# A graph layer on one core: both halves of a table from one matmul, four groups of raw rows, and the sum ahead of the node matrix

## The chip, the cores and the metric

The kernel runs on one core of a Trainium2 chip. The metric is the device time of one execution in microseconds; before the change it is 1374.2 us, the median of three runs (1370.36 to 1376.34).

## What is computed

One message-passing layer on a graph of N = 6250 nodes and E = 100000 edges, with H = 128 features and 4 attributes an edge, all in float32. The edges are sorted by destination. Cut to what matters:

```python
msg_in = concatenate([x[src], x[dst], edge_attr], axis=1)      # E x 260
h = silu(msg_in @ mW1 + mb1)                                   # E x 128
messages = h @ mW2 + mb2
aggregated = segment_sum(messages, dst, num_segments=N)        # N x 128
u = silu(concatenate([x, aggregated], axis=1) @ uW1 + ub1)
y = layer_norm(x + (u @ uW2 + ub2), ln_g, ln_b)
out = layernorm(x + y)
```

The kernel splits mW1 by rows: 128 for the source node, 128 for the destination node, 4 for the attributes. So `msg_in @ mW1` is a row of a table `x @ mW1[:128]` picked by src, plus a row of a table `x @ mW1[128:256] + mb1` picked by dst, plus a small product of the attributes. mW2 is applied after the sum over edges, folded into uW1.

## The kernel before, in words

**Groups.** Edges are worked on in groups of 1024, eight tiles of 128 edges: 98 groups. Nodes are worked on in batches of 4 tiles of 128 nodes, 13 in all, the last two shorter, each started once all edges into it are done.

**Tables.** Before the loop, TensorE transposes x, part by part (eight tiles of 128 nodes a part, seven parts, the last of one tile; `turn_x`, L325), and multiplies it with the two halves of mW1 (`product`, L318, called for part 1 at L338 and for part 0 at L341). Each call fills one PSUM buffer of 128x1024 (`wide`, three buffers in turn) with eight matmuls of 128 columns. VectorE adds mb1 to the one and SyncE's queue writes it to `tab_b` in device memory; ScalarE copies the other, which goes to `tab_a`. VectorE also clears the accumulators `acc` and `deg` (L344, L345). At 49 tiles and two halves that is 98 matmuls; the profile counts two passes each.

**Gathers.** GpSimd fetches source rows with one indirect DMA for each tile of 128 edges (`fetch`, L263, issued at L268), eight a group, into six buffers `ga`. The first RAW = 5 groups are fetched from x itself, as the tables aren't there yet; their product with mW1[:128] is made on TensorE in the loop (L563 transposes, L554 matmuls). All later groups come from `tab_a`, so the first of them waits for the last write of that table. In iteration g the loop issues the fetch of group g + 4; it can run when the buffer of group g - 2 is free, that is, when that group's rows have been read.

**The loop's iteration g** (L593 on). The program order, which is also the order on each engine's queue, since the scheduling is by hand:

- SyncE: load the destination rows of group g + 4 (`mv`, a window of 96 rows of `tab_b`) and its attributes (`st`).
- VectorE, L527 (`node_matrix`, group g + 3): a 96x1024 matrix of zeros and ones, destination window against edge, from a list of 8-bit numbers; with it, the number of edges of each node.
- TensorE, L552 (`products`, group g + 2): that matrix and the attributes times `mv`, into a PSUM buffer `pre`.
- VectorE, L570 (`hidden`, group g): `s` = gathered rows + `pre`. It is the last reader of the gather buffer. ScalarE, L571: `h` = silu(`s`).
- VectorE, L540 (`edge_matrix`, group g + 1): `oh`, edges against the window of 96, for the sum.
- TensorE, L577 and L580 (`by_nodes`, group g - 1): counts transposed, then `h` times `oh`, summed over the eight tiles into the PSUM tile `held_ps`. `oh` reads a constant row that is kept in `held_ps` too, and TensorE's L577 waits for VectorE's `oh`.
- VectorE, L586 (`add`, group g - 2): `held_ps` added into `acc` and `deg` at the window's place. It waits for TensorE's `by_nodes` just before it in the program.
- One step of each node batch that is running (`node_batch`, L394 on): matmuls, silu, two layer norms, mostly on VectorE (L411, L412, L448, L450, L457, L460) and ScalarE.

For a group of the first RAW, L565 copies the transposed rows out of PSUM in place of the sum. When iteration RAW begins, the products of three groups are made at once.

Of the kernel before, what the change touches and what calls it, by code (L numbers as in the profile page):

```python
# [8 lines left out]
F32 = mybir.dt.float32  # L9
# [9 lines left out]
P = 128  # L19
# [5 lines left out]
def kernel(  # L25
# [40 lines left out]
    nc = tc.nc  # L66
    N, H = x.shape
# [4 lines left out]
    G = 8  # L72
    GE = G * P
    NG = -(-E // GE)
# [4 lines left out]
    RB = 14  # L79
    AHEAD = 4  # L80
    LEAD = 4
    RAW = 5
    MADE = 3
    NQ = 4
    NM = 5
# [11 lines left out]
    def groups(n, g):  # L97
        return [(i, min(g, n - i)) for i in range(0, n, g)]
# [13 lines left out]
    def wide():  # L112
        return ps.tile([P, G, P], F32, name="pre", bufs=3)
# [5 lines left out]
    tpool = tables.enter_context(tc.tile_pool(name="tables", bufs=1, side="right"))  # L119
# [25 lines left out]
    x_sb = tpool.tile([P, NT, H], F32, name="x_sb")  # L145
    nf = N // P
    w1 = consts.tile([P, 2, H], F32, name="w1")
    src_l = by_group(src, 0)
    nc.scalar.dma_start(w1, mW1[: 2 * H].rearrange("(s k) f -> k s f", k=P))
    b1 = consts.tile([P, H], F32, name="b1")  # L150
# [11 lines left out]
    mv = [consts.tile([K1, H], F32, name=f"mv{k}") for k in range(NM)]  # L162
# [91 lines left out]
    tab_a = dram.tile([NP, H], F32, name="tab_a")  # L254
    tab_b = dram.tile([NW, H], F32, name="tab_b")
# [4 lines left out]
    def tiles_of(g):  # L260
        return min(G, -(-(E - g * GE) // P))

    def fetch(g):  # L263
        if g >= NG:
            return
        rows[g] = gath.tile([P, G, H], F32, name="ga")
        for i in range(tiles_of(g)):
            nc.gpsimd.indirect_dma_start(  # L268
                out=rows[g][:, i, :],
                out_offset=None,  # L270
                in_=x if g < RAW else tab_a[:, :],
                in_offset=bass.IndirectOffsetOnAxis(
                    ap=src_i[:, g, i : i + 1] if g else src_0[:, i : i + 1], axis=0
                ),
            )

    for g in range(RAW):
        fetch(g)
# [30 lines left out]
    xT = consts.tile([P, NP], F32, name="xT")  # L309

    def by_node(t):
        return t[:NP].rearrange("(i p) f -> p i f", p=P)
# [2 lines left out]
    nc.vector.memset(zeros, 0.0)  # L315
    nc.sync.dma_start(tab_b[NP:NW], zeros)

    def product(i0, n, part):  # L318
        pm = wide()
        for i in range(n):  # L320
            cols = slice((i0 + i) * P, (i0 + i + 1) * P)
            nc.tensor.matmul(pm[:, i, :], xT[:, cols], w1[:, part, :], start=True, stop=True)  # L322
        return pm[:, :n]

    def turn_x(i0, n):  # L325
        pt = wide()
        for i in range(n):
            nc.tensor.transpose(pt[:, i, :], x_sb[:, i0 + i, :], ident)
        nc.scalar.copy(xT[:, i0 * P : (i0 + n) * P], pt[:, :n, :].rearrange("p i f -> p (i f)"))
# [3 lines left out]
    for k, (i0, n) in enumerate(parts):  # L333
        if k + 1 < len(parts):
            turn_x(*parts[k + 1])

        t = x_sb[:, i0 : i0 + n, :]
        nc.vector.tensor_add(t, product(i0, n, 1), b1[:, None, :].to_broadcast([P, n, H]))  # L338
        nc.sync.dma_start(by_node(tab_b)[:, i0 : i0 + n, :], t)
        t = tpool.tile([P, G, H], F32, name="t", bufs=2)  # L340
        nc.scalar.copy(t[:, :n], product(i0, n, 0))  # L341
        nc.sync.dma_start(by_node(tab_a)[:, i0 : i0 + n, :], t[:, :n])
        cols = slice(i0 * P, NW if i0 + n == NT else (i0 + n) * P)
        nc.vector.memset(acc[:, cols], 0.0)  # L344
        nc.vector.memset(deg[:, cols], 0.0)  # L345
# [23 lines left out]
    def load_weights():  # L369
        for name, shape in (("w2", [P, H]), ("u1a", [P, H]), ("mb2", [P, 1])):  # L370
            raw_w[name] = work.tile(shape, F32, name=f"raw_{name}", bufs=1)
        nc.sync.dma_start(raw_w["w2"], mW2)
        nc.sync.dma_start(raw_w["u1a"], uW1[P:])
        nc.sync.dma_start(raw_w["mb2"], mb2.rearrange("(f o) -> f o", o=1))
        nc.sync.dma_start(u1x, uW1[:P])
        nc.sync.dma_start(u2, uW2)
        nc.sync.dma_start(ub1_col, ub1.rearrange("(f o) -> f o", o=1))
        nc.sync.dma_start(ub2_row, ub2.rearrange("(o f) -> o f", o=1))
        for t, row in ((g_b, ln_g), (b_b, ln_b)):
            nc.sync.dma_start(t, row.rearrange("(o f) -> o f", o=1).to_broadcast([P, H]))  # L380

    def fuse_weights():
        pt = narrow()
        nc.tensor.transpose(pt[:, :P], raw_w["w2"], ident)
        w2T = work.tile([P, P], F32, name="w2T", bufs=1)
        nc.scalar.copy(w2T, pt[:, :P])
        pm = narrow()
        nc.tensor.matmul(pm[:, :H], w2T, raw_w["u1a"], start=True, stop=True)
        nc.tensor.matmul(pm[0:1, H:], raw_w["mb2"], raw_w["u1a"], start=True, stop=True)
        nc.scalar.copy(w2u, pm[:, :H])  # L390
        nc.scalar.copy(mb2u, pm[0:1, H:])
# [133 lines left out]
    def node_matrix(g):  # L525

        nc.vector.tensor_scalar(  # L527
            stbuf[g % NST][:W],
            near.pop(g),
            p_next,  # L530
            0.0,
            op0=OP.is_equal,
            op1=OP.add,
            accum_out=deg_g[:, g : g + 1],
        )

    def edge_matrix(g):

        oh = work.tile([P, G, W], F32, name="oh", bufs=3)
        nc.vector.tensor_tensor(  # L540
            oh,
            w_row[:, None, :].to_broadcast([P, G, W]),
            rel[:, g, :, None].to_broadcast([P, G, W]),
            op=OP.is_equal,
        )
        return oh

    def products(g, xg=None):
        pre = wide()
        st = stbuf[g % NST].rearrange("k (i c) -> k i c", i=G)  # L550
        for i in range(tiles_of(g)):
            nc.tensor.matmul(pre[:, i, :], st[:, i, :], mv[g % NM], start=True, stop=xg is None)  # L552
            if xg is not None:
                nc.tensor.matmul(pre[:, i, :], xg[:, i, :], w1[:, 0, :], start=False, stop=True)  # L554
        return pre

    def hidden(g):
        h = hbuf[g % NH]
        ga = rows.pop(g)
        if g < RAW:  # L560
            px = wide()
            for i in range(G):
                nc.tensor.transpose(px[:, i, :], ga[:, i, :], ident)  # L563
            xg = work.tile([P, G, P], F32, name="s")
            nc.vector.tensor_copy(xg, px)  # L565
            nc.scalar.activation(h, products(g, xg), AF.Silu)
        else:
            n = tiles_of(g)
            s = work.tile([P, G, H], F32, name="s")
            nc.vector.tensor_add(s[:, :n], ga[:, :n], pre.pop(g)[:, :n])  # L570
            nc.scalar.activation(h[:, :n], s[:, :n], AF.Silu)  # L571
        return h
# [19 lines left out]
    pre, oh, h, pt, running = {}, {0: edge_matrix(0)}, {}, {}, []  # L592
    for g in range(NG + 1):  # L593
        if g == 3:
            load_weights()
        if g == 5:
            fuse_weights()
        for c in range(1, NC):
            if g == max(1, c * EC // GE - 10):
                attributes(c)  # L600
            if g == max(1, c * EC // GE - 10) + 1:
                attribute_rows(c)
        if g + AHEAD >= RAW:
            fetch(g + AHEAD)
        if g + LEAD < NG:
            load(g + LEAD)
        if g + MADE < NG:
            node_matrix(g + MADE)
        if g >= RAW:
            for k in range(g if g == RAW else g + MADE - 1, min(g + MADE, NG)):  # L610
                pre[k] = products(k)
        if g < NG - 1:
            h[g] = hidden(g)
        if g + 1 < NG:
            oh[g + 1] = edge_matrix(g + 1)
        if 0 <= g - 1 < NG:
            pt[g - 1] = by_nodes(g - 1, h.pop(g - 1), oh.pop(g - 1))
        for k in range(max(g - 2, 0), g - 1 if g < NG - 1 else g):
            if k in pt:
                add(k, pt.pop(k))  # L620
        for i0, n, first in batches:
            if g == min(first + 1, NG):
                tiles = node_tiles(nodes, node_ps)
                if first == NG:

                    tiles = (
                        nodes,
                        lambda name, p=P: gath.tile([P, G, H], F32, name="ga")[:p, :BT],
                        lambda: wide()[:, :BT],
                    )  # L630
                running.append(node_batch(i0, n, *tiles))
        advance(running)
        if g >= NG - 2:
            advance(running)
        if g == NG - 1:
            h[g] = hidden(g)
# [157 lines left out]
```

## Time and profile before

| what | value |
|---|---|
| time, median of 3 | 1374.2 us |
| profiled execution | 1372.6 us |
| busy: GpSimd / TensorE matmul / VectorE / ScalarE | 54% / 51% / 35% / 17% |
| gathers: from x, from `tab_a` | 40, 742 |
| first gather of all; last gather from x ends | 4.06 us; 54.15 us |
| first gather from `tab_a` | 88.99 us |
| last gather ends | 1297.96 us |
| matmuls of the tables (L322), passes | 196, mean 307 ns |
| sum `s` (L570), whole group | 92 times, mean 1207 ns |
| node matrix (L527) | 98 times, mean 1262 ns |

How to read it: times are counted from the first instruction. A group's line gives its engine, operation, what it writes and reads, how often, its busy time in all and for one, and after the bar how long the engine stood idle just before it, and what ended that idle time. Busy shares are means over the whole span; no engine is near full, so the order in which engines wait for each other matters more than any of the shares. A GpSimd gather is recorded with 0.95 us, and the next starts 0.30 us after it.

### The profile page before, as it was taken

To read this page: it belongs to the slowest core of one execution; us is meant where nothing else is said; L and a number is where in the kernel's file an instruction comes from. 1 tells how busy PE (TensorE), PEld (TensorE's weight loads), DVE (VectorE), ACT (ScalarE), POOL (GpSimd) and SP (SyncE) were. 2 spreads that over 40 slices of the span, in tenths; PEclk is the share of its full clock that TensorE was granted. 3 is DMA by queue.
4 is the path that set the end of the run, shared out by engine and by line. 5 is a ranking of instruction groups with operands and counts; after the bars stand their busy time and mean duration, and the time that the engine had idled before them with its cause. 6 is when DMAs were issued, how large, how long until landed. Compare 5 with 4: busy or idle time off the path is not lost. (4 is left out here: it accounts for less than half of the span.)

```text
span 1372.6 us, 11511 instructions
## 1 busy us (share of the span) xinstructions
PE 704.8 (51%) x3818; PEld 624.6 (46%) x3818; DVE 477.5 (35%) x1012; ACT 237.4 (17%) x288; POOL 741.4 (54%) x790
## 2 busy tenths in 40 slices
PE   3356743656465355445344543675543664544565
PEld 2356643545355244345234443565433454434453
DVE  1172323324334234234233325234324333225343
ACT  0121101112212112112102201212202202202223
POOL 7435564656456556546645654666655565655400
PEclk8577775755666657656656765656756665766765
DMA  6363222212312222222212221322222222222100
GB/s 168 90 177 83 56 66 65 64 48 57 79 43 67 55 60 70 58 57 70 74 33 68 56 64 41 78 58 74 62 58 58 56 69 64 58 58 56 47 1 28
DMA packets 69917, 88.96 MB, mean 65 GB/s; under 512 B 20671, under 2 KB 51534, under 8 KB 69850
## 3 DMA queue, kind: packets, MB, share of 16 engines
q0 software_dynamic: 25024, 51.30, 15.0%
q1 hardware_dynamic: 41290, 35.08, 9.0%
q10 hardware_dynamic: 3536, 1.77, 0.5%
q8 instruction: 32, 0.52, 0.1%
q14 instruction: 35, 0.29, 0.1%
HBM read 76.71 MB, written 11.38 MB: 64 GB/s over the span
## 5 line engine op out<-in xcount | busy, mean ns | idle before, releaser
L268 POOL DMA_INDIRECT ga<-tab_a,src_i x742 | 702.2, 946 | 541.6 <-DVE s L570 277.8
L552 PE MATMUL pre<-mv,st 100*128 100x128 f32 x1564 | 278.3, 336 | 57.2 <-issue 56.9
L586 DVE TENSOR_TENSOR acc<-acc,held_ps 128x96 f32 x98 | 25.0, 255 | 780.6 <-remote 511.7
L577 PE MATMUL held_ps<-ident,deg_g 96*1 96x96 f32 x98 | 28.6, 292 | 509.6 <-DVE oh L540 482.5
L552 PEld LDWEIGHTS pre<-mv,st 100*128 100x128 f32 x1564 | 257.6, 250 | 69.2 <-issue 68.8
L580 PE MATMUL held_ps<-oh,h 128*128 128x96 f32 x1564 | 287.5, 361 | 0.3 <-ACT h L571 0.3
L580 PEld LDWEIGHTS held_ps<-oh,h 128*128 128x128 f32 x1564 | 276.6, 274 | 1.4 <-ACT h L571 0.7
L577 PEld LDWEIGHTS held_ps<-ident,deg_g 96*1 96x1 f32 x98 | 8.0, 82 | 532.3 <-DVE oh L540 501.9
L571 ACT ACTIVATE h<-s 128x1024 f32<-128x1024 f32 (+1 forms) x93 | 98.1, 1055 | 718.4 <-DVE s L570 653.3
L527 DVE TENSOR_SCALAR_CACHE_REDUCE st<-near,p_next 96x1024 f32<-96x1024 uint8 x98 | 123.5, 1262 | 24.0 <-issue 14.3
L570 DVE TENSOR_TENSOR s<-ga,pre 128x1024 f32<-128x1024 f32 (+1 forms) x93 | 112.0, 1204 | 2.9 <-PE pre L552 2.7
L540 DVE TENSOR_TENSOR oh<-held_ps,rel 128x768 f32<-128x768 f32 x98 | 92.3, 942 | 0.0
L571 ACT ACT_TABLE_LOAD x21 | 26.9, 1283 | 126.0 <-DVE s L570 113.1
L322 PE MATMUL pre<-w,xT 128*128 128x128 f32 x196 | 29.1, 307 | 31.6 <-issue 15.7
L322 PEld LDWEIGHTS pre<-w,xT 128*128 128x128 f32 x196 | 27.4, 222 | 33.5 <-issue 16.0
L268 POOL DMA_INDIRECT ga<-in_x_dram,src_i x32 | 30.3, 946 | 9.8 <-issue 9.8
L554 PE MATMUL pre<-w,s 128*128 128x128 f32 x80 | 22.1, 371 | 18.9 <-DVE s L565 16.3
L417 ACT ACT_TABLE_LOAD x24 | 30.8, 1283 | 2.7 <-DVE mv L412 2.3
L446 PEld LDWEIGHTS y<-u,uT 128*128 128x128 f32 x94 | 22.7, 327 | 15.4 <-issue 15.4
L425 ACT COPY acc_b<-acc 128x512 f32<-128x512 f32 (+1 forms) x12 | 7.3, 609 | 124.3 <-DVE acc L586 115.3
L554 PEld LDWEIGHTS pre<-w,s 128*128 128x128 f32 x80 | 17.8, 275 | 19.9 <-DVE s L565 17.0
L446 PE MATMUL y<-u,uT 128*128 128x128 f32 x94 | 26.0, 448 | 0.0
(117 smaller groups left out, 396.0 us busy)
## 6 DMA issues: line engine op xcount, KB each, us to landing
ga<-tab_a,src_i POOLq DMA_INDIRECT x742
near<-near_d SPq DMA_DIRECT2D x24, 384.0 KB
mv<-tab_b SPq DMA_DIRECT2D x98, 48.0 KB
tab_b<-x_sb SPq DMA_DIRECT2D x6, 512.0 KB
tab_a<-t SPq DMA_DIRECT2D x6, 512.0 KB
xs<-in_x_dram SPq DMA_DIRECT2D x11, 256.0 KB
out_dram<-z SPq DMA_DIRECT2D x11, 256.0 KB
st<-ea_d SPq DMA_DIRECT2D x98, 16.0 KB
```

The costliest lines, as they stand in the source:

```text
L268: nc.gpsimd.indirect_dma_start(out=rows[g][:, i, :], out_offset=None, in_=x if g < RAW else tab_a[:, :], in_offset=bass.IndirectOffsetOnAx ...
L322: nc.tensor.matmul(pm[:, i, :], xT[:, cols], w1[:, part, :], start=True, stop=True)
L417: nc.scalar.activation(r[:, :n], mv[:, :n, 1], AF.Sqrt, bias=eps)
L446: nc.tensor.matmul(y[:, i, :], by_p[:, :, i], u2, start=False, stop=i == n - 1)
L527: nc.vector.tensor_scalar(stbuf[g % NST][:W], near.pop(g), p_next, 0.0, op0=OP.is_equal, op1=OP.add, accum_out=deg_g[:, g : g + 1],)
L540: nc.vector.tensor_tensor(oh, w_row[:, None, :].to_broadcast([P, G, W]), rel[:, g, :, None].to_broadcast([P, G, W]), op=OP.is_equal,)
L552: nc.tensor.matmul(pre[:, i, :], st[:, i, :], mv[g % NM], start=True, stop=xg is None)
L554: nc.tensor.matmul(pre[:, i, :], xg[:, i, :], w1[:, 0, :], start=False, stop=True)
L570: nc.vector.tensor_add(s[:, :n], ga[:, :n], pre.pop(g)[:, :n])
L571: nc.scalar.activation(h[:, :n], s[:, :n], AF.Silu)
L577: nc.tensor.transpose(pt[0:1, W:], deg_g[:, g : g + 1], ident[:W, :W])
L580: nc.tensor.matmul(pt[:, :W], h[:, i, :], oh[:, i, :], start=i == 0, stop=i == n - 1)
```

## The change

Three edits:

- *Both halves at once.* The two matmuls of 128 columns for a tile of nodes become one of 256 columns, with the transposed x loaded once. A PSUM buffer now holds both halves for four tiles; ScalarE copies the one half out and VectorE adds mb1 to the other. Both tables of a part are written once its eight tiles are done. It is for fewer weight loads and instructions on TensorE.
- *RAW from 5 to 4.* Group 4 is gathered from `tab_a`. It is for fewer transposes and matmuls in the loop, and fewer gathers ahead of the tables.
- *Sum first.* In iteration g, VectorE's sum (group g) comes ahead of the node matrix (group g + 3). It is for the gather buffer and `h` to be ready sooner.

```diff
-    RAW = 5
+    RAW = 4
...
-    def product(i0, n, part):
-        pm = wide()
-        for i in range(n):
-            cols = slice((i0 + i) * P, (i0 + i + 1) * P)
-            nc.tensor.matmul(pm[:, i, :], xT[:, cols], w1[:, part, :], start=True, stop=True)
-        return pm[:, :n]
-
...
-        t = x_sb[:, i0 : i0 + n, :]
-        nc.vector.tensor_add(t, product(i0, n, 1), b1[:, None, :].to_broadcast([P, n, H]))
-        nc.sync.dma_start(by_node(tab_b)[:, i0 : i0 + n, :], t)
-        t = tpool.tile([P, G, H], F32, name="t", bufs=2)
-        nc.scalar.copy(t[:, :n], product(i0, n, 0))
-        nc.sync.dma_start(by_node(tab_a)[:, i0 : i0 + n, :], t[:, :n])
+        tb = x_sb[:, i0 : i0 + n, :]
+        ta = tpool.tile([P, G, H], F32, name="t", bufs=2)
+        for j0, m in groups(n, G // 2):
+            pm = wide().rearrange("p (i s) f -> p i s f", s=2)
+            for j in range(m):
+                cols = slice((i0 + j0 + j) * P, (i0 + j0 + j + 1) * P)
+                nc.tensor.matmul(pm[:, j], xT[:, cols], w1, start=True, stop=True)
+            own = slice(j0, j0 + m)
+            nc.scalar.copy(ta[:, own], pm[:, :m, 0, :])
+            nc.vector.tensor_add(
+                tb[:, own], pm[:, :m, 1, :], b1[:, None, :].to_broadcast([P, m, H])
+            )
+        nc.sync.dma_start(by_node(tab_b)[:, i0 : i0 + n, :], tb)
+        nc.sync.dma_start(by_node(tab_a)[:, i0 : i0 + n, :], ta[:, :n])
...
-        if g + MADE < NG:
-            node_matrix(g + MADE)
         if g >= RAW:
             for k in range(g if g == RAW else g + MADE - 1, min(g + MADE, NG)):
                 pre[k] = products(k)
         if g < NG - 1:
             h[g] = hidden(g)
+        if g + MADE < NG:
+            node_matrix(g + MADE)
```

More of the change, by code (lines that the diff above doesn't have):

```diff
@@ L551, in products @@
         for i in range(tiles_of(g)):
-            nc.tensor.matmul(pre[:, i, :], st[:, i, :], mv[g % NM], start=True, stop=xg is None)
+            nc.tensor.matmul(
+                pre[:, i, :], st[:, i, :], mv[g % NM], start=True, stop=xg is None
+            )
             if xg is not None:
```

## The prediction

> **What bounds the kernel now.** I began with the costliest groups and the waits. No engine is full: GpSimd, the busiest, is at 54%.
>
> ```profile
> L268 POOL DMA_INDIRECT ga<-tab_a,src_i x742 | 702.2, 946 | 541.6 <-DVE s L570 277.8
> L586 DVE TENSOR_TENSOR acc<-acc,held_ps 128x96 f32 x98 | 25.0, 255 | 780.6 <-remote 511.7
> L527 DVE TENSOR_SCALAR_CACHE_REDUCE st<-near,p_next 96x1024 f32<-96x1024 uint8 x98 | 123.5, 1262 | 24.0 <-issue 14.3
> ```
>
> ```profile
> DVE acc L586 <- remote: 511.7, 40, 14.9
> POOL ga L268 <- DVE s L570: 277.8, 45, 10.5
> ```
>
> Two waits answer each other. GpSimd, which issues the gathers, waits 45 times (277.8 us) for the sum `s`, which frees a gather buffer. VectorE waits 40 times, up to 14.9 us, ahead of `acc`, for something the profile doesn't name. The timeline of two groups in mid-loop shows how they close:
>
> ```profile
> 719.64 0.95 POOL L268 DMA_INDIRECT ga<-tab_a,src_i  x1 [8.77 <-DVE s L570]
> ...
> 724.07 0.25 DVE L586 TENSOR_TENSOR acc<-acc,held_ps 128x96 f32 x1 [3.83 <-PE held_ps L580]
> ...
> 727.81 1.95 PE L580 MATMUL held_ps<-oh,h 128*128 128x96 f32 x16
> ...
> 738.42 0.95 POOL L268 DMA_INDIRECT ga<-tab_a,src_i  x1 [0.30 <-issue]
> 742.20 0.25 DVE L586 TENSOR_TENSOR acc<-acc,held_ps 128x96 f32 x1 [14.52 <-remote]
> ...
> 747.18 1.24 DVE L527 TENSOR_SCALAR_CACHE_REDUCE st<-near,p_next 96x1024 f32<-96x1024 uint8 x1
> ...
> 748.35 1.21 DVE L570 TENSOR_TENSOR s<-ga,pre 128x1024 f32<-128x1024 f32 x1
> 749.49 0.95 DVE L540 TENSOR_TENSOR oh<-held_ps,rel 128x768 f32<-128x768 f32 x1
> 749.83 0.95 POOL L268 DMA_INDIRECT ga<-tab_a,src_i  x1 [10.46 <-DVE s L570]
> 750.49 0.32 PE L577 MATMUL held_ps<-ident,deg_g 96*1 96x96 f32 x1 [18.91 <-DVE oh L540]
> ```
>
> Columns: start, duration, engine, line, and in brackets the idle time before it with what ended it. GpSimd starts 0.3 us after a sum ends (749.83), issues 16 gathers (two groups) at a pitch of 1.25 us, done at 739.37. The first `acc` of a pair comes promptly (724.07). The second needs sums whose matmuls are recorded as over at 729.76, yet it runs at 742.20, 2.83 us after GpSimd's last gather. Then VectorE does node work (left out here), L527 and the sum, and GpSimd starts again; TensorE goes on once `oh` is there (750.49). Is the release tied to GpSimd's pause, or a fixed delay? An odd pair tells:
>
> ```profile
> 297.96 3.62 PE L580 MATMUL held_ps<-oh,h 128*128 128x96 f32 x16
> ...
> 305.94 0.94 POOL L268 DMA_INDIRECT ga<-tab_a,src_i  x1 [0.30 <-issue]
> 309.58 0.26 DVE L586 TENSOR_TENSOR acc<-acc,held_ps 128x96 f32 x1 [11.80 <-remote]
> ```
>
> Here the matmuls are recorded to 301.58, so this hold is 8.0 us and not 12.4, but `acc` again runs 2.69 us after GpSimd's end (306.89). I call the wait "the hold"; what makes it I can't say. A round is thus: 16 gathers (19.7 us), 2.9 us to the release, then VectorE from `acc` to the end of `s`, in series. From 183.28 to 1297.96 GpSimd issues 686 gathers, 85.75 groups, so 13.0 us a group.
>
> Before the loop the same hold lies on the tables:
>
> ```profile
> 53.20 0.95 POOL L268 DMA_INDIRECT ga<-in_x_dram,src_i  x1 [0.30 <-issue]
> ...
> 60.51 1.01 ACT L341 COPY t<-pre 128x1024 f32<-128x1024 f32 x1 [42.94 <-remote]
> ...
> 88.99 0.95 POOL L268 DMA_INDIRECT ga<-tab_a,src_i  x1 [34.84 <-DMA mv<-in_L_gnn_mW_dram]
> ```
>
> The 40 gathers of raw rows end at 54.15; ScalarE's first copy of the tables, ready by TensorE's records at 21.2, runs at 60.51, 6.4 us after. From there the tables take 28.5 us to the first gather from them.
>
> [...]
>
> **The change, part by part.**
>
> *Sum before L527.* Nothing is added or removed; `s` (L570) moves ahead of the node matrix (L527). From L527's start to the sum's start takes 747.18 to 748.35 = 1.17 us here, 1.19 at 724.41 to 725.60: I take 1.19. That lies on the path between release and GpSimd's restart. What now waits behind `s`: L527 and `oh`. `oh` ends when it did, as the three are only permuted, so TensorE's aggregation, which waits for `oh`, moves by nothing; the products that read L527's result come one iteration later, behind that aggregation. ScalarE's `h` comes 1.2 us sooner and has an iteration of slack. GpSimd waits for the sum 45 times: 45 x 1.19 = 53.6 us, if the release stays tied to GpSimd. Lower bound 0 (release tied to TensorE's or VectorE's chain, whose sum is unchanged), upper 54.
>
> *Four raw groups.* GpSimd issues 32 gathers ahead of the tables, not 40: it ends 8 x 1.25 = 10 us sooner, at about 44, so the release comes at about 50.5 and the tables end 10 us sooner. But those 8 gathers come back behind the tables: 10 us. For group 4 an iteration loses 8 transposes and 8 matmuls and a PSUM copy (1.21 us) becomes a sum (1.21 us); TensorE's part, 0.91 (eight L563) + 16 passes x 0.11 = 2.7 us at full clock, hides behind the hold, as the raw iterations already go at 12.1 us a group (gathers at 128.10, 140.19, 152.22), the pace of eight gathers plus the pause. Net: between -10 (if iterations, which start 10 us sooner, set the pace) and 0; I take -1, GpSimd's count.
>
> *Both halves at once.* 98 matmuls of 128 columns become 49 of 256. A pass of 128 costs 0.117 us (32 passes in 3.74 us); one of 256 twice that, as I estimate from it, so 16 x 0.234 = 3.74 us a part: the same, with half the weight loads. A part runs in 4.45 us (66.69, 71.13, 75.58), of which transposes are the rest: TensorE is the bound, and VectorE (two adds of some 0.68, the row of L448's 128x512, for one of 1.23, plus 1.82 of clearing) has 3.2 us, ScalarE 2 x 0.61 (L425) + 1.0 = 2.2. Both hide. Bounds: if weights set the pass, -1.8 us a part, six parts, -11; if ScalarE and VectorE, which take each half in turn, stall TensorE, +0.7 a part, +4. I take 0.
>
> Sum: 1374.2 - 53.6 - 1 = 1319.6; 1320.
>
> **Rivals.** (a) *The wait just moves.* If the hold is TensorE's own, reordering three VectorE instructions changes nothing: 1374 - 1 = 1373. For it: 14.5 to 14.9 us recurs. Against: the pair above.
> (b) *Pairs break.* GpSimd starts 1.2 us earlier against TensorE, so the first aggregation ends 5.6 us into the gathers, not 4.4 (719.64 to 724.03). If it is then held too, only one group is freed a round: 10.0 + 2.8 + 0.4 (`acc`, `deg`) + 1.2 (sum) + 0.9 of node work (L411, L412, L448, L450, L457, L460: 90.8 us over 98 groups) = 15.3 us a group for 13.0. In 40% of 86 groups that costs 79 and loses 0.4 of the gain: 1320 + 79 + 21 = 1420, slower. For it: one first aggregation is held (ended 882.19, `acc` at 890.42), after a pause of only 1.85 us. Against: after a pause of 2.35 us (gathers from 1161.50) it went through; the pause will be about 5.
> (c) *Early releases.* In some ten rounds `acc` came before GpSimd's end (874.49 against 875.95). There GpSimd may restart almost without a pause, and the hold be longer: half the gain in a third of rounds, 1320 + 9; if it spreads, 1347.
> (d) *The tables' gain stays*: with the 10 us of the raw rows and the 11 of the passes kept to the end, 1374 - 54 - 21 = 1299. For it: the table stage is serial with the loop. Against: GpSimd has as many gathers to issue in all, and the loop's round hangs on them.
>
> **How the numbers follow.** Forecast 0.56, (a) 0.12, (b) 0.14, (c) at its worst 0.10, (d) 0.08. Predicted is the forecast's 1320. Faster: forecast, (c), (d) and a third of (a), 0.78. Within 0.5%: 0.08. Slower: (b), 0.14. The range takes in (a), (c) and nearly (d): 1298 to 1376; it leaves out (b).
>
> **What would show it.** GpSimd's pauses behind `s` shorter by 1.2 us each, their sum near 225; the hold still ending 2.9 us after its last gather; raw gathers ending at 44 and the first from the table near 78. It is wrong if `acc` comes at an unchanged distance from `oh`, or if rounds of 8 gathers replace those of 16.

## The result, and the profile after

| | before | changed |
|---|---|---|
| time, median (4 runs each) | 1372.28 us | 1329.01 us (1326.09 to 1338.05) |
| ratio, 95% interval | | 0.969 (0.964 to 0.975) |
| last gather from x ends | 54.15 us | 44.13 us |
| first gather from `tab_a` | 88.99 us | 78.64 us |
| last gather ends | 1297.96 us | 1252.75 us |
| loop: pauses of GpSimd over 1 us, sum and mean | 279.6 us, 46 of 6.08 | 239.3 us, 46 of 5.20 |

(The pauses are counted from 160 us on, from one gather's end to the next one's start.) The gain is 43 us where 54 was forecast. The lines of the page and of the waits, changed kernel (L573 and L589 are L570 and L586 of before):

```profile
L268 POOL DMA_INDIRECT ga<-tab_a,src_i x750 | 708.1, 944 | 500.5 <-DVE s L573 241.7
L573 DVE TENSOR_TENSOR s<-ga,pre 128x1024 f32<-128x1024 f32 x94 | 114.4, 1217 | 27.8 <-DMA ga<-tab_a,src_i 11.6
```

```profile
DVE acc L589 <- remote: 467.4, 39, 14.8
POOL ga L268 <- DVE s L573: 241.7, 46, 9.3
DVE s L573 <- issue: 10.4, 36, 3.4
```

The two waits that answered each other are both still there, 44 us smaller for `acc` and 36 us smaller for the gathers. A pair of groups in mid-loop, from the timeline:

```profile
717.86 3.62 PE L583 MATMUL held_ps<-oh,h 128*128 128x96 f32 x16
...
721.51 0.26 DVE L589 TENSOR_TENSOR acc<-acc,held_ps 128x96 f32 x1 [3.83 <-PE held_ps L583]
...
725.52 3.62 PE L583 MATMUL held_ps<-oh,h 128*128 128x96 f32 x16
...
734.62 0.95 POOL L268 DMA_INDIRECT ga<-tab_a,src_i  x1 [0.30 <-issue]
738.43 0.25 DVE L589 TENSOR_TENSOR acc<-acc,held_ps 128x96 f32 x1 [13.08 <-remote]
...
739.34 1.22 DVE L573 TENSOR_TENSOR s<-ga,pre 128x1024 f32<-128x1024 f32 x1 [0.21 <-issue]
740.48 1.27 DVE L528 TENSOR_SCALAR_CACHE_REDUCE st<-near,p_next 96x1024 f32<-96x1024 uint8 x1
740.83 0.94 POOL L268 DMA_INDIRECT ga<-tab_a,src_i  x1 [5.26 <-DVE s L573]
```

The first `acc` is prompt, the second comes 2.86 us after GpSimd's last gather (735.57), as before; but now the sum follows `acc`, and the node matrix (L528) runs beside GpSimd's next gathers. The pause is 5.26 us. The table stage, changed kernel:

```profile
43.18 0.95 POOL L268 DMA_INDIRECT ga<-in_x_dram,src_i  x1 [0.30 <-issue]
49.18 1.01 ACT L322 COPY xT<-pre 128x1024 f32<-128x1024 f32 x1 [10.65 <-remote]
...
78.64 0.94 POOL L268 DMA_INDIRECT ga<-tab_a,src_i  x1 [34.52 <-DMA mv<-in_L_gnn_mW_dram]
```

ScalarE's held copy runs 5.05 us after GpSimd's last raw gather, and the tables are there 10.35 us sooner.

### The profile page after: what moved, and what is told of

Its sections match the earlier page's. It is cut to its first block, busy times and chain, and to the rows that moved or that the text cites. A ratio compares the mean times of both kernels' runs of the same rounds, so it can differ in the third digit from the quotient of the medians.

```text
span 1329.3 us, 11281 instructions
## 1 busy us (share of the span) xinstructions
PE 724.5 (54%) x3696; PEld 635.2 (48%) x3696; DVE 485.1 (36%) x1018; ACT 238.8 (18%) x294; POOL 739.5 (56%) x790
## 4 chain that ended last, share of the span: by engine, by line
another core or an unknown queue 38%; DVE 25%; PE 18%; issue 14%; DMA 2%; DVEq 1%; POOL 1%; ACT 1%; SPq 0%; ACTq 0%
PE held_ps L583 11%; DVE st L528 8%; DVE oh L541 6%; DVE s L573 2%; PE pre L553 2%; DVE z L461 1%; PE pre L336 1%; DVE y L458 1%; DVE st L412 1%; POOL ga L268 1%; PE held_ps L580 1%; DVEq L573 1%; DVE deg L589 1%; DVE mv L413 1%
## 5 line engine op out<-in xcount | busy, mean ns | idle before, releaser
L268 POOL DMA_INDIRECT ga<-tab_a,src_i x750 | 708.1, 944 | 500.5 <-DVE s L573 241.7
L553 PE MATMUL pre<-mv,st 100*128 100x128 f32 x1564 | 289.2, 344 | 77.1 <-issue 76.9
L553 PEld LDWEIGHTS pre<-mv,st 100*128 100x128 f32 x1564 | 267.5, 257 | 89.7 <-issue 88.2
L583 PE MATMUL held_ps<-oh,h 128*128 128x96 f32 x1564 | 294.9, 368 | 0.3 <-ACT h L574 0.3
L589 DVE TENSOR_TENSOR acc<-acc,held_ps 128x96 f32 x98 | 24.9, 254 | 720.3 <-remote 467.4
L583 PEld LDWEIGHTS held_ps<-oh,h 128*128 128x128 f32 x1564 | 283.8, 280 | 1.3 <-ACT h L574 0.7
L574 ACT ACTIVATE h<-s 128x1024 f32<-128x1024 f32 x94 | 99.1, 1054 | 684.6 <-DVE s L573 553.6
L528 DVE TENSOR_SCALAR_CACHE_REDUCE st<-near,p_next 96x1024 f32<-96x1024 uint8 x98 | 124.2, 1269 | 1.7 <-DMA ea_d<-pad 1.7
L573 DVE TENSOR_TENSOR s<-ga,pre 128x1024 f32<-128x1024 f32 x94 | 114.4, 1217 | 27.8 <-DMA ga<-tab_a,src_i 11.6
L336 PE MATMUL pre<-w,xT 128*128 128x256 f32 x98 | 28.4, 454 | 14.6 <-issue 14.6
L336 PEld LDWEIGHTS pre<-w,xT 128*128 128x128 f32 x98 | 22.2, 233 | 19.3 <-issue 15.5
L268 POOL DMA_INDIRECT ga<-in_x_dram,src_i x24 | 22.7, 944 | 7.3 <-issue 7.3
```

The source lines that it names most:

```text
L268: nc.gpsimd.indirect_dma_start(out=rows[g][:, i, :], out_offset=None, in_=x if g < RAW else tab_a[:, :], in_offset=bass.IndirectOffsetOnAx ...
L336: nc.tensor.matmul(pm[:, j], xT[:, cols], w1, start=True, stop=True)
L528: nc.vector.tensor_scalar(stbuf[g % NST][:W], near.pop(g), p_next, 0.0, op0=OP.is_equal, op1=OP.add, accum_out=deg_g[:, g : g + 1],)
L583: nc.tensor.matmul(pt[:, :W], h[:, i, :], oh[:, i, :], start=i == 0, stop=i == n - 1)
L589: nc.vector.tensor_add(at, at, of)
```

## The experiments

Each kernel was timed on one chip beside the kernel before. The chips were not alike, and this became the main finding.

**The three edits one by one.**

```diff
# sum_first_only
-        if g + MADE < NG:
-            node_matrix(g + MADE)
...
             h[g] = hidden(g)
+        if g + MADE < NG:
+            node_matrix(g + MADE)
# raw_four_only
-    RAW = 5
+    RAW = 4
# tables_only: the changed loop over the parts, nothing else
```

> The kernel before with one edit: the sum ahead of the node matrix; five raw groups and the tables as before. Theory (the release is tied to GpSimd's pause, and the node matrix lay between release and sum): nearly all of the 43 us comes from here, so 1330 to 1340 us, GpSimd's mean pause behind the sum shorter by about 1.2 us, and the hold still ending 2.9 us after its last gather. Rival (the gain comes from the tables' 10 us and from the raw rows): 1365 to 1372 us.

> The kernel before with one edit: four raw groups for five. Theory (GpSimd has as many gathers to issue in all, and the loop's round hangs on them): the tables end 10 us sooner, the last gather of the loop only 0 to 2 us sooner, 1370 to 1372 us. Rival (the start of the loop sets its end): 10 us less, 1362 us.

> The kernel before with one edit: both halves of the table from one matmul of 256 columns. Theory (a pass of 256 costs twice one of 128): a part takes 4.3 us where it took 4.45, so about 1 us less, 1371 us. Rival (weight loads set the pass): 1.8 us less a part, 1361 us. Other rival (the two evictions of each buffer stall TensorE): 1376 us.

**The addition moved.** Its edit, on the changed kernel:

```diff
+        if g - 2 in pt:
+            add(g - 2, pt.pop(g - 2))
         if 0 <= g - 1 < NG:
             pt[g - 1] = by_nodes(g - 1, h.pop(g - 1), oh.pop(g - 1))
-        for k in range(max(g - 2, 0), g - 1 if g < NG - 1 else g):
-            if k in pt:
-                add(k, pt.pop(k))
+        if g >= NG - 1 and g - 1 in pt:
+            add(g - 1, pt.pop(g - 1))
```

> The changed kernel, with the addition of group g-2 into acc moved from behind TensorE's aggregation of group g-1 to ahead of it (behind the sum of group g), so that it waits for the aggregation of the iteration before, and the next sum isn't queued behind the newest aggregation. Theory (the aggregations queued once GpSimd runs are held until 2.9 us after its last gather): the hold stays, but VectorE frees a third group before it, so batches of 24 gathers replace 16, one pause of about 5 us for three groups: (30 + 5) / 3 = 11.7 us a group for 12.5, about 1255 us. Rival 1 (the hold is a fixed delay of about 13 us behind TensorE's instructions, whatever GpSimd does): an iteration of slack covers most of it, GpSimd runs nearly without pause, 1100 to 1150 us. Rival 2 (TensorE's own chain sets the round and the hold only fills its slack): within 10 us of 1329.

Measured, all four beside a kernel before that took **1022.89 us** and not 1372: sum first 1022.74, ratio 1.0007 (0.9996 to 1.0018); four raw groups 1028.16, 1.0062 (1.0039 to 1.0084); both halves at once (`tables_only`) 1024.83, 1.0028 (1.0018 to 1.0037); addition ahead 1025.23, 1.0033 (1.0020 to 1.0045). No theory stated for these runs had that in it. In the trace of the sum-first kernel GpSimd issues all 782 gathers, 4.07 to 982.63 us, without one pause: 1.25 us each. None of the 98 additions waits for anything unnamed. There is no hold, so nothing for the edit to shorten. The tables' edit, forecast 1 us faster, is 1.9 us slower here; its trace has one pause of GpSimd, 1.69 us at 74.5 us, behind TensorE's transposes of raw rows, where the sum-first trace has none.

**The changed kernel on two further chips.**

> The changed kernel itself once more, beside the kernel before, because in the four runs just made the kernel before took 1023 us and showed no hold at all, where it had taken 1372 us. Theory (the hold is a condition of the chip the program runs on, and the whole gain of the change hangs on it): where the kernel before takes 1023 us, GpSimd's gathers run without a pause and the changed kernel takes the same, 1020 to 1028 us; where it takes 1372 us, the changed kernel takes 1329. Rival (the parts only give their gain together): 2 to 3% faster than before, about 995 us, where the kernel before takes 1023.

> The changed kernel beside the two runs below. Theory (the gain hangs on a hold that some chips show and others don't): where the kernel before takes over 1350 us, ratio 0.97 to 0.98 with the hold 2.9 us after GpSimd's last gather; where it takes 1023 us and GpSimd issues without a pause, ratio 1.00 to 1.006. Rival (the three edits together gain on any chip): ratio under 0.99 even without the hold.

On one chip (number 3) the kernel before took 1386.44 us, the changed one 1357.77, ratio 0.980 (0.977 to 0.984), with the hold. On another (13) 1023.04 and 1029.93, ratio 1.0062 (1.0048 to 1.0075): slower. Its waits there:

```profile
DVE acc L589 <- PE held_ps L583: 330.1, 97, 5.5
...
POOL ga L268 <- issue: 225.1, 738, 0.3
DVE s L573 <- DMA ga<-tab_a,src_i: 153.2, 66, 6.1
```

Every wait for `acc` now names TensorE's aggregation (the matmuls of `h` with `oh`, 97 waits) and none is longer than 5.5 us; GpSimd waits for nothing but its own issue, 0.3 us a gather; the sum waits for gathers that are yet to land. GpSimd is the bound. Its timeline at the tables shows where the 0.6% goes:

```profile
43.10 0.95 POOL L268 DMA_INDIRECT ga<-in_x_dram,src_i  x1 [0.30 <-issue]
...
52.22 0.95 POOL L268 DMA_INDIRECT ga<-tab_a,src_i  x1 [8.17 <-DMA mv<-in_L_gnn_mW_dram]
```

With five raw groups GpSimd had gathers until 54 us, by when the tables were done; with four it stands for 8.17 us (5.56 in the kernel with that edit alone), and its last gather ends at 991.8 us instead of 982.6. So both theories for the four raw groups fall here: the edit takes work off GpSimd's list just when nothing else is ready for it.

With these went the sum-first and addition-ahead kernels again, on chip 13, where there was no hold:

> The kernel before with the sum ahead of the node matrix as its only edit. Where the hold is there: theory (the gain is that the node matrix no longer lies between release and sum): most of what the whole change gains on the same chip, at least two thirds of it, with GpSimd's mean pause behind the sum 1.0 to 1.3 us shorter. Rival (the 10 us of the table stage are the main gain): less than a third. Where the hold is not there: 1.000, as in the first run of this kernel.

> The changed kernel with the addition of group g-2 moved ahead of TensorE's aggregation of group g-1. Where the hold is there: theory (the aggregations queued once GpSimd runs are held until 2.9 us after its last gather): the sum is no longer queued behind the held addition of the same iteration, batches of 24 gathers replace 16, about 11.7 us a group for 12.5, some 70 us faster than the changed kernel. Rival 1 (a fixed delay behind TensorE's instructions): GpSimd nearly without pause, 250 us faster or more. Rival 2 (TensorE's chain sets the round): within 15 us of the changed kernel. Where the hold is not there: 1.003, as in the first run.

They gave 0.9995 (0.9986 to 1.0003) and 1.0023 (1.0014 to 1.0031). They say nothing on the hold.

**The sum first, where the hold is.**

> The kernel before with the sum ahead of the node matrix as its only edit, on a further chip. Where the hold is there: theory (the gain is that the node matrix no longer lies between release and sum): ratio 0.970 to 0.983, as the changed kernel on such chips (0.969 and 0.980), with GpSimd's pauses behind the sum 1.0 to 1.3 us shorter on average. Rival (the table stage's 10 us are the gain, or the three edits only gain together): 0.99 or more. Where the hold is not there: 1.000, as twice before.

On chip 3 again: before 1381.96 us, sum first alone 1344.83, ratio 0.975 (0.971 to 0.978). The same chip had given the whole change 0.980 (0.977 to 0.984). The edit alone gains 37.1 us, the whole change 28.7, in two sittings. The two intervals just meet, at 0.977 to 0.978: all of the gain is the sum's place, and the other two edits added nothing there; whether they cost some microseconds isn't settled. The waits of this kernel:

```profile
DVE acc L586 <- remote: 497.0, 43, 13.5
...
POOL ga L268 <- DVE s L570: 252.5, 49, 9.5
```

GpSimd's mean wait behind the sum is 5.15 us, 1.02 less than before's 6.17 (the trace of before is from the result's chip).

**Sum first and addition ahead, where the hold is** (the two edits above, on the kernel before).

> The kernel before with two edits: the sum ahead of the node matrix, and the addition of group g-2 ahead of TensorE's aggregation of group g-1; five raw groups and tables as before. Where the hold is there: theory (what is queued on TensorE once GpSimd runs is held until 2.9 us after its last gather): the sum is no longer queued behind the newest, held aggregation, batches of 24 gathers and more replace those of 16, ratio 0.88 to 0.93. Rival 1 (a fixed delay behind TensorE's instructions, whatever GpSimd does): GpSimd nearly without pause, ratio under 0.82. Rival 2 (TensorE's own chain sets the round): ratio 0.96 to 0.98, as the changed kernel. Where the hold is not there: GpSimd issues its 782 gathers without a pause, ratio 0.997 to 1.002, where the changed kernel, with four raw groups, took 1.006.

On a chip (12) with the hold: 1368.92 and 1335.30 us, ratio 0.977 (0.973 to 0.981). The gain of the addition's move, forecast at some 70 us, isn't there. The timeline says why:

```profile
300.06 0.94 POOL L268 DMA_INDIRECT ga<-tab_a,src_i  x1 [4.98 <-DVE s L570]
...
305.07 1.95 PE L580 MATMUL held_ps<-oh,h 128*128 128x96 f32 x16
...
318.83 0.94 POOL L268 DMA_INDIRECT ga<-tab_a,src_i  x1 [0.30 <-issue]
...
321.87 0.96 DVE L540 TENSOR_TENSOR oh<-held_ps,rel 128x768 f32<-128x768 f32 x1 [10.85 <-remote]
```

The wait went over to `oh`, which stands ahead of `acc` now and reads its constant row from the tile `held_ps`, so it waits for the aggregation last written there: 629.2 us in 44 waits. I had overlooked this wait. So the run doesn't refute the theory behind the move. But it holds a comparison that turned out to be worth more. What waits for this aggregation, recorded as over at 307.02, only 7 us after GpSimd's start, is held until GpSimd's end (319.77 + 2.1). With it TensorE had begun 86 instructions since 300.06, weight loads counted.

**Fewer TensorE instructions.** So I counted, in the four traces with the hold that have the addition in its old place, the TensorE instructions since GpSimd's start (the first gather after a pause of over 1 us, from 160 us on) up to the end of each aggregation. From 34 to 53 of them (187 aggregations): `acc` came within 1 us of the aggregation's recorded end in 173, mostly 0.04 us after it; the other 14 all follow a pause of only 1.1 to 2.3 us. From 100 to 166 (159): 3.3 to 12.8 us late, every one; 113 of these additions ran 2.4 to 3.4 us after GpSimd's last gather, 32 before it. In between lay three, at the change from raw groups to the table: at 75, 77 and 94, late by 6.4, 6.2 and 2.1 us. The theory on record for the addition's move spoke of what is queued; the next kernel tries the count. It writes `h` and `oh` in bfloat16, which changes the rounding of the sum over edges: an aggregation then has 18 instructions for 34, and its matmuls of `h` with `oh` are 8 passes (1122.45 below) for 16 (305.07 above).

```diff
 # on the kernel with the sum first
-        hbuf.append(held.tile([P, G, H], F32, name=f"h{k}"))
+        hbuf.append(held.tile([P, G, H], mybir.dt.bfloat16, name=f"h{k}"))
...
-        oh = work.tile([P, G, W], F32, name="oh", bufs=3)
+        oh = work.tile([P, G, W], mybir.dt.bfloat16, name="oh", bufs=3)
```

> The kernel before with the sum ahead of the node matrix, and with h and oh written in bfloat16, which changes the rounding of the aggregation: one pass a tile for two, so an aggregation is 18 TensorE instructions (weight loads counted) for 34, and a group 50 for 66. Theory (in the traces with the hold, results of TensorE come at once up to about 55 instructions after GpSimd starts a batch, at some microseconds late near 67, and always late from 101 on: the count decides): the second aggregation of a round moves from instruction 102 to about 70, is held by 1 to 5 us and not by 9, VectorE frees a third group before GpSimd ends, batches of 24 replace 16: ratio 0.90 to 0.94 where the hold is there. Rival 1 (the time since GpSimd's start decides, not the count): 0.970 to 0.978, as with the sum first alone. Rival 2 (any second aggregation is held until GpSimd ends): the same. Where the hold is not there: 0.995 to 1.002, GpSimd's gathers set the end.

> The same kernel (sum ahead of the node matrix; h and oh in bfloat16, which changes the rounding of the aggregation) on a further chip, as the first showed no hold. Where the hold is there: theory (the count of TensorE instructions since GpSimd starts a batch decides): the second aggregation of a round ends at about instruction 70 and not 102, is held by 1 to 5 us and not by 9, batches of 24 gathers replace 16: ratio 0.90 to 0.94. Rival 1 (time since GpSimd's start) and rival 2 (any second aggregation is held until GpSimd ends): 0.970 to 0.978, as with the sum first alone. Where the hold is not there: 0.990 to 0.993, as before.

First on chip 13, without a hold: 1014.82 us, 0.9915 (0.9902 to 0.9929); the gathers end at 982.1 as ever, and the work after them is shorter. Then on chip 11, with the hold: 1381.39 and 1291.60 us, ratio 0.932 (0.927 to 0.937). Of 33 batches in the loop 21 are of 24 gathers and the rest shorter; with the sum alone none was longer than 16. A round of three groups:

```profile
1115.28 0.95 POOL L268 DMA_INDIRECT ga<-tab_a,src_i  x1 [6.00 <-DVE s L570]
...
1118.13 0.26 DVE L586 TENSOR_TENSOR acc<-acc,held_ps 128x96 f32 x1 [1.05 <-PE held_ps L580]
...
1122.45 0.50 PE L580 MATMUL held_ps<-oh,h 128*128 128x96 bf16 x8
...
1124.40 0.26 DVE L586 TENSOR_TENSOR acc<-acc,held_ps 128x96 f32 x1 [2.09 <-PE y L430]
...
1128.37 0.50 PE L580 MATMUL held_ps<-oh,h 128*128 128x96 bf16 x8
...
1132.89 0.37 PE L552 MATMUL pre<-mv,st 100*128 100x128 f32 x1 [1.82 <-issue]
1134.98 0.37 PE L552 MATMUL pre<-mv,st 100*128 100x128 f32 x1 [1.72 <-issue]
...
1147.62 0.37 PE L552 MATMUL pre<-mv,st 100*128 100x128 f32 x1 [1.03 <-issue]
...
1149.20 0.26 DVE L586 TENSOR_TENSOR acc<-acc,held_ps 128x96 f32 x1 [20.97 <-remote]
```

The second aggregation is now at instruction 70 of the batch, and its `acc` comes 1.45 us after it (22 such cases, median 0.50 us, the longest 8.4), in place of about 9. The third, at 133, is held to 4.2 us after GpSimd's end (1145.0). Count or time? The 22 at instruction 70 ended 7.3 to 9.1 us after GpSimd's start. Ten more in this kernel, at some 90, ended at 10.0 to 11.2 and were late by 8.6 to 12.4 us, which fits either. The one of the kernel with both edits, at 86, ended at 7.0; there are six of its kind there, ended at 6.7 to 7.3, and they were late by 1.7, 6.9 and four times 13 to 16 us. Earlier by the clock and later by the count, most of them were held longer. These six speak for the count and against the time alone. They are few, they wait at `oh` and not at `acc`, and they come from another chip; and instructions and matmul passes go together in all these kernels, so which of the two is counted isn't shown. Nor is the count sharp: after a pause of some 2 us an aggregation can be held at 35, as if what is left of the batch before counted too.

**Two rivals that the kept traces can settle.** The first is that TensorE waits for its own program to be fetched. It comes by queue q8, which the profile lists as `instruction`, as far as the counts tell: q8's packets of 16 KB fall from 32 to 26 where bfloat16 takes away some 1570 instructions, and the other queue of instructions, q14, keeps its 35. A packet takes 0.9 to 1.6 us in the bfloat16 kernel with the hold and 0.9 to 1.7 us in the sum-first kernel without it, and none is under way between 1090.5 and 1154.5 us, where the round above lies. The second is that memory is busier: the gathers' packets have a median of 102 ns in the kernel before, with the hold, and of 104 ns in the sum-first kernel without it. Neither explains the hold.

The bfloat16 kernel's gain of 90 us is not all the hold's: the stretch from the first table gather to the last gather is 1142.6 us for 1178.1 with the sum alone, 36 us less, and the end behind it 59 for 74, 16 us less. A group costs 12.28 us from 166 us on, for 12.70. (The two ran on chips 11 and 3, where the kernel before took 1381 and 1382 us.)

## Why the prediction was right, point by point

*What bounds the kernel: the hold.* Right for the chip it was read on. That it belongs to the program was taken for granted, and is not so: beside the result, and on chips 3 (twice), 11 and 12, the kernel before took 1369 to 1386 us; on chips 6 and 13 (twice) 1023 us, the same program. The kernels traced there show the same pitch of gathers and no hold. Nothing in the one profile could have told that. On chips 6 and 13 the forecast would have missed; that the result's chip is of the kind that the profile came from owes nothing to the reasoning, and is luck.

*What the hold is.* The prediction left this open. The theory that went on record with the addition's move was that the aggregations queued once GpSimd runs are held until 2.9 us after its last gather. The runs correct it: with bfloat16 the second aggregation of a batch, at instruction 70, begun 7.2 us after GpSimd's start in the round above (1122.45 for 1115.28), still went through within 1 us in 15 of 22 cases. When an instruction is queued, no trace shows. What the delays follow is a number of instructions, or of the passes that go with them, from GpSimd's start on, and they set in at about 70. The lines of 1132.89 to 1147.62 show more: while GpSimd issues, TensorE's instructions come in steps of 0.70 us, twice that or, seldom, three times (a weight load between two matmuls), where earlier in the round, at 1125.72, sixteen matmuls and their sixteen weight loads take 2.05 us; this goes on until 3 to 4 us after the last gather. In eleven batches of that kernel the slow steps begin at recorded instruction 137 to 149, some 70 behind the count from which results are late. What makes that distance isn't shown.

The steps mark the hold in every trace: from 90 us on, 52 to 152 pairs of TensorE instructions start 0.65 to 0.75 us apart in the six traces with the hold, and 3 to 6 in the eight without.

Why some chips do this stays open: no trace or run here shows a cause.

*Sum before L527, 45 x 1.19 = 53.6 us.* The mechanism was right: the release comes 2.9 us after GpSimd's last gather in the median of the late aggregations, the sum right behind it, the node matrix off the path; alone it gave 0.975. The term was too large. The 46 pauses shrank from 279.6 to 239.3 us, 40.3 us, 0.88 each. The full 1.19 took for granted that nothing would stand ahead of the sum once the node matrix was gone. The sum's own idle time is 27.8 us where it was 2.9: 11.6 in six waits for gathers yet to land, and otherwise mostly 0.13 to 0.21 us at a time behind `deg` or node work, a gap that used to lie under the node matrix (before, only three sums had more than 0.05). That is enough for the 13.3 us missing, though not all of it need lie in GpSimd's pauses. GpSimd's wait for the sum was forecast near 225 and is 241.7.

*Four raw groups, net -10 to 0, taken as -1.* The instants were right: gathers ending at 44 (44.13), the first from the table near 78 (78.64). So was the net, as far as it can be followed: at the first gather of group 6, which both kernels fetch from the table, the changed kernel is 0.37 us ahead (98.63 for 99.00), as the eight gathers more took up the 10.35 us gained. What the edit does to the later loop with the hold was not run alone. Where there is no hold it costs 5 us, outside the bounds: GpSimd, with no hold to wait for, runs out of gathers before the tables are there.

*Both halves at once, 0.* Right: a part's 16 passes take 3.62 us (3.74 forecast) and a part 4.3 (4.45 before). Without the hold the edit alone cost 1.9 us; with the hold it was not run alone.

*The sum of the terms.* From group 6's first gather to the last gather the changed kernel takes 44.8 us less (1154.1 for 1199.0), and what follows the last gather 1.9 us more: with the 0.37 that is the 43.3 us between the two profiled runs. It lies nearly all in the loop, where the prediction had it.

*The rivals.* (a) fell: `acc` moved with GpSimd's end. (b) didn't occur: the first aggregations, at instruction 35, ended 5.6 us after GpSimd's start and nearly all went through, which fits that their count had not changed. (c) has the measured time at its near end, but not the reason: pauses of 1 to 3.1 us are six where there were five, and the missing microseconds lie in ordinary pauses. (d) fell: of the tables' 10.35 us, 0.37 are left at group 6.

## What to carry to other kernels

When a wait ends at a fixed distance from another engine's last instruction, here 2.9 us in the median, whatever lies between that release and the other engine's restart is on the path. Moving it out can be worth less than its full length, here 0.88 of 1.19 us a pause, since what follows brings its own waits. A wait without a named releaser can belong to the chip and not to the program: run the kernel before on a second chip before building on it; here the same change is 3% faster on one, 2% faster on another and 0.6% slower on a third. An instruction that reads a constant out of a tile that another engine keeps writing can inherit that engine's waits: here `oh` waited 629 us in 44 waits.

## What the runs showed of the hardware

- While GpSimd issues indirect gathers at a pitch of 1.25 us, on the result's chip and on chips 3, 11 and 12, what waits for a TensorE result is released late from some 70 TensorE instructions of a batch on: mostly 0.04 us after the recorded end at 34 to 53 instructions, 3.3 to 12.8 us after it at 100 to 166. Where TensorE has more to do (1132.89 to 1147.62 us above), its recorded starts fall to one per 0.70 us or slower, until 3 to 4 us after the last gather. On chips 6 and 13 there is no such stretch, and the kernel before takes 1023 us for 1369 to 1386.
- An aggregation recorded as over at 307.02 us released the instruction that waited for it at 321.87: a release can come 15 us after the recorded end without any mark on TensorE's own rows.
- The best version with the hold, sum first with a bfloat16 aggregation, which changes the rounding, is also the fastest without it (1291.6 and 1014.8 us), though there GpSimd's 782 gathers of 1.25 us, 978 us, are the floor: they end at 982.1 us.
